# Six layers of windowed attention on one core: both halves of the product with V in one block, and K's projection split around P's transposes

## The chip, the cores and the metric

The kernel runs on one core of a Trainium2 chip. The metric is the device time in microseconds of one execution; lower is better. Times are medians of the runs named. Engines are called TensorE (PE; PEld is its weight load), VectorE (DVE), ScalarE (ACT), GpSimd (POOL) and SyncE (SP, which here only issues DMAs).

## The reference, cut to what matters

The input is x of shape (4, 512, 128), float32. First comes a full attention with 16 heads of 64 and a residual, then a second residual around six layers, each a windowed attention and a gated FFN:

```python
x = x + attn(layernorm(x), Wq, Wk, Wv, Wr)          # 16 heads, full softmax over 512 keys
h = layernorm(x)
for i in range(6):
    t = shift_tokens(h)                              # half of the features come from the token before
    q, k, v = split(t @ Wqkv[i])                     # 128 -> 3 x 1024
    q, k = rotary(l2norm(q) * qs[i]), rotary_inv(l2norm(k) * ks[i])
    p = softmax(8 * q @ k2.T + band)                 # windows of 32 queries, 64 keys: own window and the one before
    h = (p @ v2) @ Wo[i] + h                         # 1024 -> 128
    t = layernorm(shift_tokens(h)) * g + b
    a, gate = split(t @ W1[i] + b1)                  # 128 -> 2 x 341
    h = (a * gelu(gate)) @ W2[i] + b2 + h
x = x + h
```

## The kernel before

There are two stages in one program, with instruction order on every engine written out by hand. The first stage (to about 568 us) is the full attention; the change does not touch it. The second stage is the six layers.

**Units and slots.** A unit is 128 tokens of one layer: 6 layers x 4 batch entries x 4 tiles = 96 units, numbered in that order. Activations lie transposed, features on partitions. The work is a software pipeline: `slot(n)` emits, in this order, parts of four units: scores and the exponential of unit n; the projections, rotation and norms of unit n+2 (`new`); the transposes of Q and K of unit n+1 (`nxt`); and the output projection and residual of unit n-1 (`prev`). The FFN of a finished batch entry (four units) is spread over the following seven slots in three lists, `move` (the token shift), `norm` (mean, variance, scale, one a slot) and `geglu` (three chunks of 128 of the inner width, then the output). After unit n-1, with n a multiple of four, the shift is in slot n, the mean in n+1, the variance in n+2, the scale in n+3, the chunks in n+3 to n+5, the output in n+6.

**One slot on TensorE before.** Scores: eight bf16 matmuls that lay the band mask (L652), then 128 float32 matmuls of 64x32 tiles (L663). Q's projection (L517; one half of 512 columns is two matmul records in the trace). The norm's step, if the slot has one (L97, L106 or L114). Output projection of the unit before (L720, 16 records). P's eight transposes in two groups of four (L625, from `pr`). K's projection. First half of the product with V (`times_v(u, 0)`, L695, 64 matmuls of 64x32 tiles). Q's eight transposes (L625, from `rot`). V's projection. Second half of the product (`times_v(u, 1)`). K's eight transposes. The FFN's chunk (L763, L764) or output (L783). The eight transposes of the product (L625, from `on`).

**The other engines.** VectorE reduces the scores to maxima (L673) and subtracts them (L675), adds the residual (L728), rotates Q and K in two operations each (L538, L542), sums their squares (L533) and divides the product by the softmax sums (L704, L705, once per half). ScalarE does the exponential (L681), the squares (L528), all copies of transposes out of PSUM (L628), V's copies (L607) and the FFN's gelu (L767). GpSimd adds the two parts of a rotation (L553), scales Q and K by their inverse norms (L561) and does the Newton steps of inverse roots (L84 to L87); the two integer operations that start a root (L81, L82) are on VectorE. SyncE issues sixteen copies per unit which spread V into windows (L615 to L619), used two slots later.

**PSUM.** Three tiles of two banks, `two0` to `two2`, and two tiles of one bank, taken in turn by `one_t`. `two_t(k)` takes tile (part + k) mod 3, and `part` is set at the start of every slot:

```python
part[0] = n % 3
```

In a slot, scores take k=0, Q's projection 1, K's 2, both halves of the product 0, V's projection 1, the FFN 2. `one_t` serves, in turn: the norm's step, the output projection's y, P's two groups, Q's two, K's two, the product's two. With two such tiles, P's second group takes the one that held y, which L728 must have read.

Of the kernel before, what the change touches and what calls it, by code (L numbers as in the profile page):

```python
# [15 lines left out]
P = 128  # L16
# [16 lines left out]
def body(ctx: ExitStack, tc: tile.TileContext, a, out: bass.AP):  # L33
# [54 lines left out]

    def layernorm_steps(state, bank, inT, outT, g=None, b=None, eng=nc.vector, nt=NT, temp=tmpt):

        w = nt * P

        def mean():
            m = bank()[:, 0:w]
            mm(m, lhsT=avg, rhs=inT(), start=True, stop=True)  # L97
            xc = state["xc"] = temp()[:, 0:w]
            nc.vector.tensor_tensor(xc, inT(), m, ALU.subtract)
            sq = state["sq"] = temp()[:, 0:w]  # L100
            nc.scalar.activation(sq, xc, AF.Square)

        def var():
            v = bank()
            for t in range(nt):
                mm(v[:, t : t + 1], lhsT=state["sq"][:, t * P : (t + 1) * P], rhs=avg[:, 0:1], start=True, stop=True)  # L106
            rs = state["rs"] = small.tile([P, NT], F32, tag="rs", name="rs")[:, 0:nt]
            nc.vector.tensor_scalar(rs, v[:, 0:nt], EPS, None, ALU.add)  # L108
            rsqrt(rs, nt, eng)

        def scale():
            bc = bank()[:, 0:w]
            for t in range(nt):
                nc.tensor.transpose(  # L114
                    bc[:, t * P : (t + 1) * P], state["rs"][:, t : t + 1].to_broadcast([P, P]), ident
                )
            h = state["h"] = outT()
            nc.vector.tensor_tensor(h, state["xc"], bc, ALU.mult)
            if g is not None:
                nc.vector.tensor_scalar(h, h, g, b, ALU.mult, ALU.add)  # L120

        return mean, var, scale
# [390 lines left out]

    def project(u, j):
        p = two_t((1, 2, 1)[j], "ps_proj")
        for c in range(2):
            mm(  # L517
# [5 lines left out]
            )  # L523
        return flat(p)

# [8 lines left out]

    def rotate(u, j):
        t0 = u.r[j] = s2a.tile([P, INNER], F32, tag="rot", name="rot", bufs=6)
        lt, pf, half = u.lt, u.p[j], HD // 2
        nc.vector.tensor_tensor(  # L538
            heads(t0), heads(pf), lt[:, u.T, 2 * j].unsqueeze(1).to_broadcast([P, HEADS, HD]), ALU.mult
        )  # L540
        t1 = u.t1 = s2a.tile([P, INNER], F32, tag="t1", name="t1", bufs=3)
        nc.vector.tensor_tensor(  # L542
# [139 lines left out]

    def transpose_p(u):
        u.pT = s2.tile([P, NC, P], F32, tag="pT", name="pT", bufs=2)
        for g in range(2):
            transposed(u.prf, g, u.pT, 0)

    def times_v(u, g, k=0):
        if g == 0:
            u.on = s2.tile([P, NC, 2, HD], F32, tag="on", name="on", bufs=1)  # L690
        o = two_t(k, "ps_att")
        for c in range(4):
# [40 lines left out]
    class Ffn:  # L733
        def __init__(self, u, t0=0, nt=NT, temp=tmpt, pair=None, eng=None):
            self.i, self.b, self.u, self.t0, self.nt, self.us, self.st = u.i, u.b, u, t0, nt, [], {}
# [9 lines left out]
                nt,  # L745
                temp,
            )

# [84 lines left out]

    def do_project(u, j):
        u.p[j] = project(u, j)
        if u.b + 1 == B and u.T + 1 == NT and u.i + 1 < L:
            wpart[j] = load_part(u.i + 1, j)
# [25 lines left out]
    def slot(n, norm, move, geglu):  # L863
# [4 lines left out]
        u, prev, nxt, new = unit(n), unit(n - 1), unit(n + 1), unit(n + 2)  # L868
        part[0] = n % 3
        begin(unit(n + 4))  # L870
# [16 lines left out]
        for f in move:  # L887
            f()
        if u:
            transpose_p(u)  # L890
        if new:
# [5 lines left out]
        if new:  # L897
            do_project(new, 1)
            square(new, 1)
        if u:  # L900
            times_v(u, 0)
        if nxt:
            transpose_q(nxt)
        if new:
            do_project(new, 2)
            v_windows(new, follower(new))
            rotate(new, 1)
            add_rotated(new, 1)
        if u:
            times_v(u, 1)  # L910
        if new:
            sum_squares(new, 1)
        if nxt:
# [14 lines left out]
    with tc.manual_schedule():  # L928
        begin(units[0])
        late = norm_x1(one_t, B - 1)  # L930


        norm, move, geglu = {}, {}, {}

# [7 lines left out]
        for n in range(NT, end - NT, NT):  # L942
            f = Ffn(units[n - 1], eng=nc.gpsimd)
            plan(move, n, f.shift)
            for k, g in enumerate((f.mean, f.var, f.scale)):
                plan(norm, n + 1 + k, g)
            for k in range(3):
                plan(geglu, n + 3 + k, at(f.chunk, k, 2))
            plan(geglu, n + 6, at(f.out, 2, n + 6 == end - 2))
        third, seq = f, Ffn(units[end - NT - 1], eng=nc.gpsimd)  # L950
# [26 lines left out]
        def tail():  # L977
# [5 lines left out]
            most.shift()  # L983
            transpose_p(u)
            most.mean()
            part[0] = 1
            times_v(u, 0, 0)
            times_v(u, 1, 1)
            part[0] = 0
# [26 lines left out]
        for n in range(-1, end - 1):  # L1016
            if 1 <= n < 4:
                late[n - 1]()
            slot(n, norm.get(n, ()), move.get(n, ()), geglu.get(n, ()))
# [94 lines left out]
```

## Time and profile before

| | |
|---|---|
| three runs | 2259.30, 2260.88, 2263.07 us; median 2260.88 |
| profiled execution | 2261.35 us; its span from first to last instruction 2259.6 us |
| granted TensorE clock | 0.993 of full speed |
| TensorE busy in the span | 2183.4 us |
| VectorE, ScalarE, GpSimd busy | 1710.3, 1365.9, 1511.7 us |
| slots of the layers (start of one L652 to the next) | 96 from 568.5 us on; usual lengths 16.3, 17.2, 18.5, 17.0 us for n mod 4 = 0, 1, 2, 3 |

The profile is one execution. A row of its order of time gives start, busy time, engine, line, operation, the tiles written and read, shape and count, and in brackets how long the engine was idle before and what ended it. Matmuls overlap one another in the pipe and their ends are modelled, so for TensorE the distance from one start to the next says more than the busy time.

### The profile page before, as it was taken

To read this page: it belongs to the slowest core of one execution; us is meant where nothing else is said; L and a number is where in the kernel's file an instruction comes from. 1 tells how busy PE (TensorE), PEld (TensorE's weight loads), DVE (VectorE), ACT (ScalarE), POOL (GpSimd) and SP (SyncE) were. 2 spreads that over 40 slices of the span, in tenths; PEclk is the share of its full clock that TensorE was granted. 3 is DMA by queue.
4 is the path that set the end of the run, shared out by engine and by line. 5 is a ranking of instruction groups with operands and counts; after the bars stand their busy time and mean duration, and the time that the engine had idled before them with its cause. 6 is when DMAs were issued, how large, how long until landed. Compare 5 with 4: busy or idle time off the path is not lost.

```text
span 2259.6 us, 82472 instructions
## 1 busy us (share of the span) xinstructions
PE 2183.4 (97%) x35150; PEld 1435.4 (64%) x35150; DVE 1710.3 (76%) x2501; ACT 1365.9 (60%) x2589; POOL 1511.7 (67%) x2281
## 2 busy tenths in 40 slices
PE   7999999999899999999999999999999999999997
PEld 5565655554666666666666666666666666666665
DVE  4676667676778888878788788878888788888874
ACT  4665656564556656666566656666566666666663
POOL 2554545465787777777777777777777777777762
PEclk8999999999999999999999999999999999999999
DMA  3000000000322233232322323223232223322221
GB/s 117 1 1 1 1 1 1 1 1 9 75 69 60 69 87 73 57 76 69 85 69 62 78 66 86 66 67 73 71 85 63 66 71 87 76 63 70 60 67 28
DMA packets 91064, 125.77 MB, mean 56 GB/s; under 512 B 25422, under 2 KB 39500, under 8 KB 90700
## 3 DMA queue, kind: packets, MB, share of 16 engines
q1 hardware_dynamic: 89996, 118.79, 21.4%
q8 instruction: 280, 4.59, 0.9%
q10 hardware_dynamic: 704, 1.70, 0.2%
q14 instruction: 84, 0.69, 0.1%
HBM read 20.31 MB, written 1.05 MB: 9 GB/s over the span
## 4 chain that ended last, share of the span: by engine, by line
PE 58%; DVE 12%; POOL 3%; issue 2%; ACT 1%; POOLq 0%; ACTq 0%
PE ps_proj L517 18%; PE ps_one L625 14%; PE ps_att L663 6%; PE ps_att L695 6%; PE ps_one L720 3%; PE ps_proj L783 3%; PE ps_proj L763 3%; PE ps_proj L764 3%; DVE y L82 2%; DVE mx L673 2%; DVE pr L675 2%; PE ps_att L652 1%; DVE hT L120 1%; POOL rot L553 1%; DVE t L542 1%
## 5 line engine op out<-in xcount | busy, mean ns | idle before, releaser
L553 POOL TENSOR_TENSOR rot<-rot,t 128x1024 f32<-128x1024 f32 x192 | 453.9, 2365 | 255.8 <-DVE t L542 188.5
L517 PE MATMUL ps_proj<-wqkv,xs 128*128 128x512 f32 x1152 | 557.0, 606 | 5.9 <-DVE tmp_t L771 5.0
L344 POOL TENSOR_TENSOR pr<-pr,den 128x1024 f32<-128x1024 f32 x128 | 241.0, 1894 | 247.5 <-DVE den L341 239.6
L561 POOL TENSOR_TENSOR rot<-rot,ss 128x1024 f32<-128x1024 f32 x192 | 361.5, 1904 | 7.4
L517 PEld LDWEIGHTS ps_proj<-wqkv,xs 128*128 128x128 f32 x1152 | 197.5, 191 | 157.2 <-issue 143.2
L528 ACT ACTIVATE sq<-ps_proj 128x1024 f32<-128x1024 f32 x192 | 195.3, 1017 | 127.5 <-PE ps_proj L517 126.8
L681 ACT ACTIVATE pr<-pr 128x1024 f32<-128x1024 f32 x96 | 101.5, 1058 | 260.8 <-DVE pr L675 260.8
L542 DVE TENSOR_TENSOR t<-ps_proj,lt 128x1024 f32<-128x1024 f32 x192 | 233.2, 1215 | 19.6 <-POOL rot L553 19.2
L538 DVE TENSOR_TENSOR rot<-ps_proj,lt 128x1024 f32<-128x1024 f32 x192 | 233.0, 1214 | 19.5 <-ACT sq L528 19.4
L533 DVE TENSOR_REDUCE ss<-sq 128x16 f32<-128x1024 f32 x192 | 231.6, 1206 | 0.0
L330 ACT ACTIVATE pr<-ps_sc,nm 128x128 f32<-128x128 f32 (+3 forms) x448 | 220.6, 511 | 5.7 <-DVE nm L317 5.2
L317 DVE TENSOR_REDUCE nm<-ps_sc 128x2 f32<-128x1024 f32 x128 | 155.9, 1218 | 82.8 <-PE ps_sc L305 82.7
L673 DVE TENSOR_REDUCE mx<-ps_att 128x16 f32<-128x1024 f32 x96 | 117.5, 1224 | 127.1 <-PE ps_att L663 127.1
L625 PE MATMUL ps_one<-ident,rot 128*128 128x128 f32 x1536 | 209.6, 279 | 0.9 <-POOL rot L561 0.9
L720 PEld LDWEIGHTS ps_one<-aT,wo 128*128 128x128 f32 x1536 | 183.0, 192 | 24.6 <-issue 23.9
L720 PE MATMUL ps_one<-aT,wo 128*128 128x128 f32 x1536 | 189.1, 276 | 0.4 <-DVE rs L108 0.3
L625 PEld LDWEIGHTS ps_one<-ident,rot 128*128 128x128 f32 x1536 | 164.7, 141 | 19.8 <-POOL rot L561 1.1
L695 PEld LDWEIGHTS ps_att<-vw,pT 64*32 64x32 f32 x9216 | 101.1, 105 | 108.3 <-issue 108.0
L607 ACT COPY vt<-ps_proj 128x512 f32<-128x512 f32 x192 | 103.2, 590 | 101.3 <-PE ps_proj L517 101.3
L355 PEld LDWEIGHTS ps_pt<-ident,pr 128*128 128x128 f32 x1024 | 118.2, 142 | 56.9 <-issue 47.1
L84 POOL TENSOR_TENSOR yt<-y 128x32 f32<-128x32 f32 (+2 forms) x384 | 88.0, 229 | 93.6 <-DVE y L82 47.5
L355 PE MATMUL ps_pt<-ident,pr 128*128 128x128 f32 x1024 | 135.7, 275 | 3.0 <-POOL pr L344 2.7
(173 smaller groups left out, 4083.0 us busy)
## 6 DMA issues: line engine op xcount, KB each, us to landing
vw<-vt SPq DMA_DIRECT2D x1152, 65.0 KB, 2.0
vw_first<-vt SPq DMA_DIRECT2D x336, 65.0 KB, 2.0
wqkv<-in_wqkv_dram SPq DMA_DIRECT2D x18, 512.0 KB, 9.2
wo<-in_wo_dram SPq DMA_DIRECT2D x6, 512.0 KB
w<-in_w_dram SPq DMA_DIRECT2D x6, 341.0 KB, 3.5
xr<-in_x_dram SPq DMA_DIRECT2D x3, 256.0 KB
scales<-in_scales_dram SPq DMA_DIRECT2D x6, 128.0 KB, 3.2
w<-in_w_dram SPq DMA_DIRECT2D x12, 64.0 KB, 2.9
```

Source lines behind the costliest of these rows:

```text
L330: nc.scalar.activation(self.pr[:, h, cols], self.sc[:, h, cols], AF.Exp, bias=self.nm[:, part_, h : h + 1], accum_out=self.den[:, part_, h ...
L344: nc.gpsimd.tensor_tensor(self.pr, self.pr, self.den[:, 0].unsqueeze(2).to_broadcast([P, 2, S]), ALU.mult)
L355: nc.tensor.transpose(pt[:, k * P : (k + 1) * P], self.pr[:, h, k * P : (k + 1) * P], ident)
L517: mm(p[:, c, :], lhsT=u.xs[:, u.T * P : (u.T + 1) * P], rhs=wpart[j][:, c * 512 : (c + 1) * 512], start=True, stop=True,)
L533: nc.vector.tensor_reduce(u.ss[:, j * HEADS : (j + 1) * HEADS], heads(u.sq), AX.X, ALU.add)
L538: nc.vector.tensor_tensor(heads(t0), heads(pf), lt[:, u.T, 2 * j].unsqueeze(1).to_broadcast([P, HEADS, HD]), ALU.mult)
L542: nc.vector.tensor_tensor(t1.rearrange("p (h t d) -> p h t d", t=2, d=half), pf.rearrange("p (h t d) -> p h t d", t=2, d=half)[:, :, ::-1, :],
L553: nc.gpsimd.tensor_tensor(u.r[j], u.r[j], u.t1, ALU.add)
L561: nc.gpsimd.tensor_tensor(heads(u.r[j]), heads(u.r[j]), u.ss[:, j * HEADS : (j + 1) * HEADS].unsqueeze(2).to_broadcast([P, HEADS, HD]), AL ...
L625: nc.tensor.transpose(tp[:, c * P : (c + 1) * P], src[:, (4 * g + c) * P : (4 * g + c + 1) * P], ident)
L695: mm(o[j * W : (j + 1) * W, h, c * (HD + 1) : (c + 1) * (HD + 1)], lhsT=u.pT[h * HD : (h + 1) * HD, 4 * g + c, j * W : (j + 1) * W], rhs=u ...
L720: mm(y[:, 0:P], lhsT=wo_w[0][:, c, :], rhs=u.aT[:, c, :], start=(c == 0), stop=(c == NC - 1))
```

## The change

Nine things change, all in the layers' stage; no arithmetic is added or left out.

1. K's projection is split into its two halves of 512 columns. One half is emitted ahead of P's second group of transposes (in slots with no norm step ahead of both groups), the other behind them. In slot 0 the whole of it comes ahead.
2. Both halves of the product with V are emitted one after the other, into tiles 0 and 1 of the slot.
3. V's projection, which stood between them, comes behind them and behind Q's transposes, into tile 0, the tile of the product's first half. K's rotation (VectorE) comes ahead of it in the text, behind the product's division.
4. The tiles turn the other way: `part` is (-1 - n) mod 3, and the FFN takes tile 1 instead of 2.
5. Three operations of the FFN's norm, the square (L101), the root (L81 to L87) and the gain and offset (L120), are put on a list and emitted between the two operations that rotate K.
6. The norm of the last batch entry ahead of the layers is emitted inside slots 0, 1 and 2 rather than ahead of slots 1, 2 and 3.
7. The sum of K's squares comes directly behind K's rotation.
8. In the last layer the transposes and the store of a finished batch entry come one slot after the FFN's output rather than directly behind it.
9. In slot 0, Q's transposes come ahead of the product.

```diff
-        p = two_t((1, 2, 1)[j], "ps_proj")
-        for c in range(2):
+    def project(u, j, c0=0, c1=2):
+        p = u.p[j] if c0 else two_t(((1, 2, 1), (0, 2, 1), (1, 2, 0))[min(u.n, 2)][j], "ps_proj")
+        u.p[j] = p
+        for c in range(c0, c1):
...
-    def rotate(u, j):
+    def rotate(u, j, between=()):
...
+        for f in between:
+            f()
         t1 = u.t1 = s2a.tile([P, INNER], F32, tag="t1", name="t1", bufs=3)
...
-            nc.scalar.activation(sq, xc, AF.Square)
+            then(lambda: nc.scalar.activation(sq, xc, AF.Square))
...
-            rsqrt(rs, nt, eng)
+            then(lambda: rsqrt(rs, nt, eng))
...
-                nc.vector.tensor_scalar(h, h, g, b, ALU.mult, ALU.add)
+                then(lambda: nc.vector.tensor_scalar(h, h, g, b, ALU.mult, ALU.add))
...
-        part[0] = n % 3
+        part[0] = (-1 - n) % 3
...
+        if n == 0:
+            do_project(new, 1)
         if u:
-            transpose_p(u)
+            if norm:
+                transpose_p(u, 0)
+        if new and n != 0:
+            do_project(new, 1, 0, 1)
+        if u:
+            if not norm:
+                transpose_p(u, 0)
+            transpose_p(u, 1)
         if new:
             rotate(new, 0)
             add_rotated(new, 0)
...
         if new:
-            do_project(new, 1)
+            if n != 0:
+                do_project(new, 1, 1)
             square(new, 1)
+        if nxt and n == 0:
+            transpose_q(nxt)
         if u:
             times_v(u, 0)
-        if nxt:
+            times_v(u, 1)
+        if new:
+            rotate(new, 1, later)
+            later.clear()
+            add_rotated(new, 1)
+            sum_squares(new, 1)
+        if nxt and n != 0:
             transpose_q(nxt)
         if new:
             do_project(new, 2)
             v_windows(new, follower(new))
-            rotate(new, 1)
-            add_rotated(new, 1)
-        if u:
-            times_v(u, 1)
-        if new:
-            sum_squares(new, 1)
         if nxt:
             transpose_k(nxt)
...
-                plan(geglu, n + 3 + k, at(f.chunk, k, 2))
-            plan(geglu, n + 6, at(f.out, 2, n + 6 == end - 2))
+                plan(geglu, n + 3 + k, at(f.chunk, k, 1))
+            ends = f.i + 1 == L
+            plan(geglu, n + 6, at(f.out, 2 if n + 6 == end - 2 else 1, ends))
+            if ends and n + 6 < end - 2:
+                plan(geglu, n + 7, f.finish)
```

In `times_v` the tile is now `two_t(g, "ps_att")`, g being the half.

More of the change, by code (lines that the diff above doesn't have):

```diff
@@ L87, in rsqrt, with layernorm_steps, then @@
             eng.tensor_tensor(y if k < 2 else v, y, t, ALU.mult)
-    def layernorm_steps(state, bank, inT, outT, g=None, b=None, eng=nc.vector, nt=NT, temp=tmpt):
+    def layernorm_steps(state, bank, inT, outT, g=None, b=None, eng=nc.vector, nt=NT, temp=tmpt, later=None):
         w = nt * P
+        def then(f):
+            f() if later is None else later.append(f)
         def mean():
@@ L512, in __init__ @@
             self.r = [None, None]
-    def project(u, j):
-        p = two_t((1, 2, 1)[j], "ps_proj")
-        for c in range(2):
+    def project(u, j, c0=0, c1=2):
+        p = u.p[j] if c0 else two_t(((1, 2, 1), (0, 2, 1), (1, 2, 0))[min(u.n, 2)][j], "ps_proj")
+        u.p[j] = p
+        for c in range(c0, c1):
             mm(
@@ L523, in project @@
             )
-        return flat(p)
+        if c1 == 2:
+            u.p[j] = flat(p)
     def square(u, j):
@@ L681, in exponents, with transpose_p, times_v @@
         nc.scalar.activation(u.prf, u.prf, AF.Exp)
[L683 to L688, printed above, removed]
+    def transpose_p(u, g):
+        if g == 0:
+            u.pT = s2.tile([P, NC, P], F32, tag="pT", name="pT", bufs=2)
+        transposed(u.prf, g, u.pT, 0)
+    def times_v(u, g):
         if g == 0:
             u.on = s2.tile([P, NC, 2, HD], F32, tag="on", name="on", bufs=1)
-        o = two_t(k, "ps_att")
+        o = two_t(g, "ps_att")
         for c in range(4):
@@ L733, in body, with __init__ @@
     class Ffn:
-        def __init__(self, u, t0=0, nt=NT, temp=tmpt, pair=None, eng=None):
+        def __init__(self, u, t0=0, nt=NT, temp=tmpt, pair=None, eng=None, later=None):
             self.i, self.b, self.u, self.t0, self.nt, self.us, self.st = u.i, u.b, u, t0, nt, [], {}
@@ L746, in __init__ @@
                 temp,
+                later,
             )
@@ L832, in begin, with do_project @@
             v.xs, v.lt, v.p = xs, lt, [None] * 3
-    def do_project(u, j):
-        u.p[j] = project(u, j)
-        if u.b + 1 == B and u.T + 1 == NT and u.i + 1 < L:
+    def do_project(u, j, c0=0, c1=2):
+        project(u, j, c0, c1)
+        if c1 == 2 and u.b + 1 == B and u.T + 1 == NT and u.i + 1 < L:
             wpart[j] = load_part(u.i + 1, j)
@@ L929, in body @@
         begin(units[0])
+        later = []
         late = norm_x1(one_t, B - 1)
-        norm, move, geglu = {}, {}, {}
+        norm, move, geglu = {k: [f] for k, f in enumerate(late)}, {}, {}
         def plan(steps, n, *fs):
@@ L942, in body @@
         for n in range(NT, end - NT, NT):
-            f = Ffn(units[n - 1], eng=nc.gpsimd)
+            f = Ffn(units[n - 1], eng=nc.gpsimd, later=later)
             plan(move, n, f.shift)
@@ L983, in tail @@
             most.shift()
-            transpose_p(u)
+            transpose_p(u, 0)
+            transpose_p(u, 1)
             most.mean()
             part[0] = 1
-            times_v(u, 0, 0)
-            times_v(u, 1, 1)
+            times_v(u, 0)
+            times_v(u, 1)
             part[0] = 0
@@ L1016, in body @@
         for n in range(-1, end - 1):
-            if 1 <= n < 4:
-                late[n - 1]()
             slot(n, norm.get(n, ()), move.get(n, ()), geglu.get(n, ()))
```

## Prediction

> **What bounds the kernel now.** I read the engine totals first, then the waits, then TensorE's own order of time in one layer slot.
>
> The page's totals, and its TensorE rows over 40 slices:
>
> ```profile
> PE 2183.4 (97%) x35150; PEld 1435.4 (64%) x35150; DVE 1710.3 (76%) x2501; ACT 1365.9 (60%) x2589; POOL 1511.7 (67%) x2281
> ...
> PE   7999999999899999999999999999999999999997
> PEld 5565655554666666666666666666666666666665
> ```
>
> TensorE is full from end to end; nothing else is near it. So a change that removes no arithmetic gains only what TensorE loses between instructions. Those losses do not show as idle time, because a matmul's record runs on while the pipe empties. I therefore count from start to start. TensorE in order of time (start, busy, line, count, idle before and who ended it), one slot of 17.02 us, from L652 up to the FFN's first half (eight transposes of the product, 0.97 us, end it):
>
> ```profile
> 1311.90 0.41 PE L652 MATMUL ps_att<-band,ident 64*32 64x512 bf16 x8
> 1312.12 1.72 PE L663 MATMUL ps_att<-kT,qT 64*32 64x64 f32 x128
> 1313.77 1.98 PE L517 MATMUL ps_proj<-wqkv,xs 128*128 128x512 f32 x4
> 1315.59 0.60 PE L114 MATMUL ps_one<-ident,rs 128*128 128x128 f32 x4
> 1316.03 1.95 PE L720 MATMUL ps_one<-aT,wo 128*128 128x128 f32 x16
> 1317.81 0.60 PE L625 MATMUL ps_one<-ident,pr 128*128 128x128 f32 x4
> 1318.67 0.66 PE L625 MATMUL ps_one<-ident,pr 128*128 128x128 f32 x4 [0.26 <-DVE xT L728]
> 1319.16 1.88 PE L517 MATMUL ps_proj<-wqkv,xs 128*128 128x512 f32 x4
> 1320.98 0.86 PE L695 MATMUL ps_att<-vw,pT 64*32 64x65 f32 x64
> 1321.77 1.09 PE L625 MATMUL ps_one<-ident,rot 128*128 128x128 f32 x8
> 1322.70 1.88 PE L517 MATMUL ps_proj<-wqkv,xs 128*128 128x512 f32 x4
> 1324.51 0.86 PE L695 MATMUL ps_att<-vw,pT 64*32 64x65 f32 x64
> 1325.30 1.09 PE L625 MATMUL ps_one<-ident,rot 128*128 128x128 f32 x8
> 1326.23 1.02 PE L763 MATMUL ps_proj<-hT,w 128*128 128x512 f32 x2
> 1327.09 1.02 PE L764 MATMUL ps_proj<-hT,w 128*128 128x512 f32 x2
> ```
>
> Two losses are seen. First, P's eight transposes take 1.35 us (1317.81 to 1319.16), while four of L114 take 0.44, so eight should take 0.88. Second, each block of 64x32 tiles (L695) costs something at both ends: four projection matmuls take 1.82 us ahead of it and 1.72 elsewhere (L763 with L764), and the eight transposes behind it take 0.93 instead of 0.88.
>
> Who delays P: the same stretch on VectorE and GpSimd (first three rows one slot earlier), and the totals by waiter (us, times, longest):
>
> ```profile
> 1298.62 1.91 POOL L561 TENSOR_TENSOR rot<-rot,ss 128x1024 f32<-128x1024 f32 x1
> 1298.71 1.83 DVE L82 TENSOR_SCALAR y<-yt 128x4 int32<-128x4 int32 x1
> 1300.46 0.28 DVE L728 TENSOR_TENSOR xT<-ps_one,xT 128x128 f32<-128x128 f32 x1
> ...
> 1317.15 1.27 DVE L120 TENSOR_SCALAR hT<-hT,vecs 128x512 f32<-128x512 f32 x1
> ```
>
> ```profile
> PEld ps_one L625 <- DVE xT L728: 32.6, 69, 1.7
> ...
> PE ps_one L625 <- DVE xT L728: 17.5, 44, 1.4
> ```
>
> The second four of P need the bank that holds y until L728 has added the residual. L728 stands on VectorE behind the norm's little operations, and L82 on 128x4 took 1.83 us because it ended with GpSimd's L561; elsewhere it takes 0.18.
>
> **The change part by part.** Classes are slots by n mod 4: class 1 does the norm's mean, 2 its variance and the FFN's output, 3 its scale, 0 no norm. S is a slot's start, E the end of its L720 block.
>
> *P's wait.* Over 95 slots, start to start, P's blocks and the steps into them exceed 0.11 us per transpose by 8.1 us in class 0, 4.0 in class 1, 16.7 in class 2, 11.2 in class 3: 40.1 in all. Class 0 is another wait: P comes 0.26 us ahead of the exponential's end (S+5.61). Afterwards half of K's projection (two matmuls at 0.43, 0.86 us) stands ahead of P's second four, and in class 0 ahead of P altogether. L82 and L120 are behind L728 now, so L728 ends near E+0.5, and P's second four come at E+1.30. Covered everywhere, by 0.8 us; class 0's exponential by 0.7. Minus 40.1 us. Splitting K removes no matmul and repeats none, so the split itself is nothing.
>
> *One block.* This takes away one switch into small tiles and one out. Into: 0.523 against 0.429 us from the last projection matmul, 0.094. Out: the first transpose step takes 0.165 against 0.109, 0.056. The two blocks take 0.79 each from first to follower; how a joint block runs is to be seen once, in the tail of before:
>
> ```profile
> 2227.94 1.59 PE L695 MATMUL ps_att<-vw,pT 64*32 64x65 f32 x128
> 2229.46 1.12 PE L763 MATMUL ps_proj<-hT,w 128*128 128x512 f32 x2
> ```
>
> That is 1.52 for 1.58, 0.063. Together 0.213 us by 95 slots, minus 20.2. The Trainium skill, "TensorEngine Tiling (Array Packing)", Key Properties, says that a change of tiling mode drains the engine. By that rule alone I would price the switch at what a matmul's record has left after its follower's turn: 0.592-0.429 in, and 0.217-0.010 out, 0.37 a slot, minus 35. The rows show cheaper switches, and the joint block in the tail stands for itself; I take 20.2, and keep 6 (a joint block as slow as scores, 1.65) to 35 as ends.
>
> The Trainium skill's "Perfetto Trace Analysis", Identifying the Most-Contended Engine, calls matmul busy share a bad measure of room on TensorE. This bears on the sum: idle time by the busy rows is 196 of each 200 us, 2% of the 1650 us of layers, so at most 33 us; the start-to-start count finds 60. I use the latter.
>
> *V behind the product, tiles turned.* V's projection goes into the tile of the product's first half, so it waits for that half's division (L704, L705). TensorE after E: P 0.44, K 0.86, P 0.44, K with the switch 0.95, the product 1.52, Q's transposes 0.93: V is due at E+5.14. VectorE from L538 on: steps of 1.15, 1.13, 1.13, 0.23 and L705's 0.69, 4.33 us. L538 starts at E+0.4 in classes 1 and 2, so L705 ends at E+4.75: no wait. In class 3 L538 starts at S+6.64, E+0.73: E+5.06, just in time. In class 0 L538 cannot start before ScalarE's square of the same tile ends (S+6.55, E+1.03): E+5.36, with 0.05 for the signal and 0.1 for an exposed weight load 0.37 us late, 24 times: plus 8.9. The product's second half needs L542 of Q done, at E+3.1 to E+3.4, and is due at E+3.41: nothing. Turning the tiles the other way puts scores on the tile of the previous K (L542 done by E+8.5, scores at E+10.4), Q on the previous V's, K on the FFN's: all released earlier than needed; the waits of L517 for L771 (5 us on PE) are included in P's margin.
>
> *The rest of the moved work.* L120 now stands between K's two rotations, in class 3 at E+6.95; GpSimd is between its two L553 then, so it should take the 0.55 us of its shortest record on 128x512 rather than the usual 1.37, and end at E+7.5; the FFN's first matmul is due at E+7.73. If it were blocked again: 0.6 us in 23 slots, 14 us; I keep that for the range. The norm's root on GpSimd (12 small operations, 3.3 us) now delays K's L553 and so the next unit's scaling by up to 3 us in class 2; Q's transposes still have over 2 us. V's projection moves from E+4.9 to E+5.1, so the sixteen window copies on SP's queue (0.5 to 1.3 us each, wanted two slots later) move by as little. At a layer's start the scales' load stands behind them and lt's product holds GpSimd; slots 45 and 61 took 20.8 and 21.5 us for 17.2. With shorter slots this bites earlier: nothing to 2 us at each of five starts, I take 4 in all. The final transposes moved out of slot 90 (21.58 us for 18.4 in its class; four transposes come back in slot 91): minus 2.5. In slot 0 K's whole projection fills part of a 2.3 us wait for the exponential: minus 1.5.
>
> Sum: -40.1-20.2+8.9+4-2.5-1.5 = -51.4. The profiled execution is 2261.35 us (span 2259.6), 0.5 above the median of the three runs, 2260.88: 2209.5.
>
> **The rivals.**
> *VectorE's ring takes over* (21 in 100). Per slot VectorE is busy about 14 us of 17, and L557 will now be blocked behind K's L553 for about 1 us, where a division stood before. If it is late by 0.3 us per slot at scores or at V, 28 us come back: 2237. For it: its margin before scores falls from 1.1 to 0.2-0.5 us by the rows. Against: it now idles 127.1 us in all for scores.
> *Nothing comes back* (10 in 100): class 0's wait doesn't show and a joint block costs less: 2190.
> *V waits for the whole product* (7 in 100), the slower side. If V is released only by the second half's L705 (0.95 us later: E+5.7 to E+6.3), it is 0.6 to 1.3 us late in every slot, with the load about 1.0, 95 us: 2296. The break-even is a new wait of 0.68 us per slot (64.3/95). Against it: VectorE runs in order, and the first half's L705 is counted first.
>
> **How the numbers follow.** My forecast has 62 in 100, 2196 to 2224 by itself. The range takes in most of the second and third case: 2191 to 2240. This kernel's runs tell 0.2% apart, 4.5 us; only the slower case or part of the second reaches there: faster 0.90, same 0.03, slower 0.07.
>
> **What would show it.** P's two groups of four at 0.44 us each without a wait for the residual; one block of 128 L695 matmuls of about 1.5 us; slots of 16.3, 16.8, 17.5, 16.3 us by class; a VectorE wait ahead of V's projection in class 0 only. Wrong if that wait is in all classes, if FFN matmuls wait for hT, or if slots keep their length.

## The result and the profile after

Before: 2261.57 us (2259.30 to 2263.07). After: 2227.98 us (2223.71 to 2230.22). The ratio is 0.9853, with a 95% interval of 0.9840 to 0.9867: 33.6 us less, where the forecast said 51.4. The profiled execution of after took 2230.15 us, its span 2228.3.

The page's totals of after, and TensorE's rows over 40 slices:

```profile
PE 2153.5 (97%) x35150; PEld 1438.0 (65%) x35150; DVE 1704.1 (76%) x2501; ACT 1358.5 (61%) x2589; POOL 1510.9 (68%) x2281
...
PE   7999999999889999999999999999999999999997
PEld 5555655555566666666666666666666666666665
```

The number of matmuls is the same, and TensorE is as full as before, so the 31.3 us of span have gone from between its instructions, as the forecast wanted. (After's line numbers are higher: band L659, scores L670, projections L521, output projection L727, transposes L632, product L702, FFN L771, L772 and L791; on VectorE maxima L680, rotation L543 and L549, sums L538, division L711 and L712, residual L735.) TensorE in order of time, in after, from P's first group to V's projection; a slot of class 3, the same slot number 43 as shown of before:

```profile
1303.32 0.60 PE L632 MATMUL ps_one<-ident,pr 128*128 128x128 f32 x4
1303.76 1.02 PE L521 MATMUL ps_proj<-wqkv,xs 128*128 128x512 f32 x2
1304.62 0.60 PE L632 MATMUL ps_one<-ident,pr 128*128 128x128 f32 x4
1305.06 1.02 PE L521 MATMUL ps_proj<-wqkv,xs 128*128 128x512 f32 x2
1306.01 1.74 PE L702 MATMUL ps_att<-vw,pT 64*32 64x65 f32 x128
1307.68 1.09 PE L632 MATMUL ps_one<-ident,rot 128*128 128x128 f32 x8
1308.61 1.89 PE L521 MATMUL ps_proj<-wqkv,xs 128*128 128x512 f32 x4
```

P's groups are 0.44 us from start to follower (1303.32 to 1303.76, 1304.62 to 1305.06) with no wait behind either; before, the two took 1.35 together here. The product is one block. Here it took 1.67 us with its follower; its median in this class is 1.45.

The same rows in the next slot, class 0:

```profile
1319.31 1.02 PE L521 MATMUL ps_proj<-wqkv,xs 128*128 128x512 f32 x2
1320.17 1.04 PE L632 MATMUL ps_one<-ident,pr 128*128 128x128 f32 x8
1321.05 1.02 PE L521 MATMUL ps_proj<-wqkv,xs 128*128 128x512 f32 x2
1322.00 1.87 PE L702 MATMUL ps_att<-vw_first,pT 64*32 64x65 f32 x128
1323.80 1.09 PE L632 MATMUL ps_one<-ident,rot 128*128 128x128 f32 x8
1324.98 1.99 PE L521 MATMUL ps_proj<-wqkv,xs 128*128 128x512 f32 x4
```

Two new losses are seen without any bracket: the product takes 1.80 us instead of 1.44, and Q's eight transposes 1.18 (1323.80 to 1324.98) instead of 0.93. The totals of the waits of after on TensorE:

```profile
PE ps_att L702 <- issue: 11.8, 10, 2.7
PE ps_att L670 <- issue: 8.8, 10, 1.9
...
PE ps_one L632 <- DVE xT L735: 1.4, 1, 1.4
```

P's wait for the residual, 17.5 us in 44 places before, is one place of 1.4 us. New on top is a wait of the product for "issue", nothing that the profile shows; before it had 0.9 us, once.

From start to start, summed by operation over slots 0 to 94 (us):

| operation | before | after |
|---|---|---|
| P's transposes | 115.8 | 86.6 |
| output projection | 174.4 | 171.2 |
| projections of Q, K, V | 517.7 | 508.0 |
| product with V | 153.3 | 163.2 |
| transposes of Q and K | 181.9 | 194.7 |
| scores | 164.0 | 155.5 |
| the rest (norm, FFN, other transposes, band) | 342.0 | 334.5 |
| sum | 1649.1 | 1613.7 |

That is -35.4; the first scores begin 2.7 us later than before (571.2 for 568.5) and the tail is 1.5 us longer. A typical slot, taken as the sum of the medians of its operations (so were the lengths given of before), has 16.40, 16.86, 17.49 and 16.31 us in classes 0 to 3, where the forecast said 16.3, 16.8, 17.5 and 16.3. The whole slots have medians of 16.42, 17.00, 17.50 and 16.33 and means of 16.43, 17.14, 17.63 and 16.74: the typical slot was forecast well, and something irregular was not.

### The profile page after: what moved, and what is told of

It is laid out like the page before. It is cut to its first block, busy times and chain, and to the rows that moved or that the text cites. A ratio compares the mean times of both kernels' runs of the same rounds, so it can differ in the third digit from the quotient of the medians.

```text
span 2228.3 us, 82460 instructions
## 1 busy us (share of the span) xinstructions
PE 2153.5 (97%) x35150; PEld 1438.0 (65%) x35150; DVE 1704.1 (76%) x2501; ACT 1358.5 (61%) x2589; POOL 1510.9 (68%) x2281
## 4 chain that ended last, share of the span: by engine, by line
PE 50%; DVE 14%; POOL 6%; issue 4%; ACT 2%; POOLq 0%; ACTq 0%
PE ps_proj L521 15%; PE ps_one L632 10%; PE ps_one L727 5%; PE ps_att L670 5%; PE ps_att L702 4%; DVE t L549 3%; DVE ss L538 3%; PE ps_proj L791 3%; PE ps_proj L771 2%; PE ps_proj L772 2%; DVE rot L543 2%; POOL rot L568 2%; POOL rot L560 2%; DVE pr L682 1%; DVE mx L680 1%
## 5 line engine op out<-in xcount | busy, mean ns | idle before, releaser
L560 POOL TENSOR_TENSOR rot<-rot,t 128x1024 f32<-128x1024 f32 x192 | 454.1, 2367 | 198.7 <-DVE t L549 165.8
L521 PE MATMUL ps_proj<-wqkv,xs 128*128 128x512 f32 x1152 | 573.6, 607 | 5.2 <-issue 1.6
L568 POOL TENSOR_TENSOR rot<-rot,ss 128x1024 f32<-128x1024 f32 x192 | 361.6, 1905 | 7.5
L521 PEld LDWEIGHTS ps_proj<-wqkv,xs 128*128 128x128 f32 x1152 | 189.5, 191 | 122.3 <-issue 102.8
L543 DVE TENSOR_TENSOR rot<-ps_proj,lt 128x1024 f32<-128x1024 f32 x192 | 233.8, 1218 | 31.3 <-ACT sq L533 31.0
L549 DVE TENSOR_TENSOR t<-ps_proj,lt 128x1024 f32<-128x1024 f32 x192 | 233.5, 1216 | 29.4 <-POOL rot L560 29.4
L538 DVE TENSOR_REDUCE ss<-sq 128x16 f32<-128x1024 f32 x192 | 232.0, 1208 | 0.0
L632 PEld LDWEIGHTS ps_one<-ident,rot 128*128 128x128 f32 x1536 | 173.0, 141 | 66.7 <-issue 53.9
L632 PE MATMUL ps_one<-ident,rot 128*128 128x128 f32 x1536 | 206.1, 277 | 6.3 <-issue 2.1
L727 PEld LDWEIGHTS ps_one<-aT,wo 128*128 128x128 f32 x1536 | 184.4, 193 | 23.7 <-issue 23.0
L727 PE MATMUL ps_one<-aT,wo 128*128 128x128 f32 x1536 | 190.7, 278 | 0.4 <-DVE rs L111 0.3
L680 DVE TENSOR_REDUCE mx<-ps_att 128x16 f32<-128x1024 f32 x96 | 117.3, 1222 | 74.4 <-PE ps_att L670 74.3
L635 ACT COPY qT<-ps_one 128x512 f32<-128x512 f32 x192 | 103.5, 589 | 111.7 <-PE ps_one L632 111.7
L635 ACT COPY pT<-ps_one 128x512 f32<-128x512 f32 x192 | 109.9, 586 | 75.3 <-PE ps_one L632 75.1
```

The source lines that it names most:

```text
L521: mm(p[:, c, :], lhsT=u.xs[:, u.T * P : (u.T + 1) * P], rhs=wpart[j][:, c * 512 : (c + 1) * 512], start=True, stop=True,)
L538: nc.vector.tensor_reduce(u.ss[:, j * HEADS : (j + 1) * HEADS], heads(u.sq), AX.X, ALU.add)
L543: nc.vector.tensor_tensor(heads(t0), heads(pf), lt[:, u.T, 2 * j].unsqueeze(1).to_broadcast([P, HEADS, HD]), ALU.mult)
L549: nc.vector.tensor_tensor(t1.rearrange("p (h t d) -> p h t d", t=2, d=half), pf.rearrange("p (h t d) -> p h t d", t=2, d=half)[:, :, ::-1, :],
L560: nc.gpsimd.tensor_tensor(u.r[j], u.r[j], u.t1, ALU.add)
L568: nc.gpsimd.tensor_tensor(heads(u.r[j]), heads(u.r[j]), u.ss[:, j * HEADS : (j + 1) * HEADS].unsqueeze(2).to_broadcast([P, HEADS, HD]), AL ...
```

## Where the new losses are

**The division of the product's first half.** V's projection waits for its tile, and that for L712 on VectorE. In class 0 (VectorE in order of time, after, slot 44, which starts at 1313.90):

```profile
1320.52 1.23 DVE L543 TENSOR_TENSOR rot<-ps_proj,lt 128x1024 f32<-128x1024 f32 x1 [0.71 <-ACT sq L533]
1321.66 1.22 DVE L549 TENSOR_TENSOR t<-ps_proj,lt 128x1024 f32<-128x1024 f32 x1
...
1324.15 0.69 DVE L712 TENSOR_TENSOR on<-ps_att,rden 128x512 f32<-128x512 f32 x1
```

L543 starts late, behind ScalarE's square (the bracket). The product's second half needs L549's tile, and L549 ends at 1322.88, 0.88 us into a product that began at 1322.00: its second 64 matmuls, due after some 0.72, stand. L712 ends at 1324.84, and V starts at 1324.98. In medians over the class: 0.36 in the product, 0.25 behind Q's transposes, 0.07 in V's first weight load, 0.68 us a slot.

In class 1 the cause is one slot earlier. VectorE of after, the end of slot 36 and slot 37 (which starts at 1195.08):

```profile
1192.83 1.23 DVE L549 TENSOR_TENSOR t<-ps_proj,lt 128x1024 f32<-128x1024 f32 x1 [1.27 <-POOL rot L560]
...
1195.21 1.39 DVE L564 TENSOR_SCALAR ss<-ss 128x32 f32<-128x32 f32 x1
...
1197.07 0.74 DVE L779 SCALAR_TENSOR_TENSOR tmp_t<-ps_proj,vecs,tmp_t 128x512 f32<-128x512 f32 x1
1197.73 1.21 DVE L680 TENSOR_REDUCE mx<-ps_att 128x16 f32<-128x1024 f32 x1
...
1202.24 1.23 DVE L543 TENSOR_TENSOR rot<-ps_proj,lt 128x1024 f32<-128x1024 f32 x1 [0.29 <-ACT sq L533]
...
1205.87 0.69 DVE L712 TENSOR_TENSOR on<-ps_att,rden 128x512 f32<-128x512 f32 x1
```

K's second rotation L549 waited 1.27 us for GpSimd's add L560, which stood behind two token shifts (1187.61 to 1190.35): the next units' and the FFN's, both in slots of class 0. So the operations behind it come late: L564, which takes 1.38 or 1.39 us beside GpSimd's next L560 in classes 0 to 2 alike (medians), starts 0.1 us into the slot in class 1, against 0.8 and 1.2 ahead of it in classes 0 and 2. The gate L779 runs into the new slot, and the maxima begin 2.65 us into it instead of about 2.07. The exponential, the square behind it and so L543 come late; L712 ends at 1206.56, and V, which was due 0.93 us behind the start of Q's transposes (1205.58 + 0.93 = 1206.51), starts at 1206.71. In medians 0.27 us a slot. Class 3 loses 0.19, since the joint block is faster than forecast and V is due sooner. Class 2 loses nothing. Together 0.68 x 24 + 0.27 x 24 + 0.19 x 23 = 27.2 us, by medians.

**Stops inside a run of small matmuls.** TensorE of after, two product blocks:

```profile
1508.86 1.46 PE L702 MATMUL ps_att<-vw,pT 64*32 64x65 f32 x122
1513.05 0.43 PE L702 MATMUL ps_att<-vw,pT 64*32 64x65 f32 x6 [2.73 <-issue]
...
1886.46 1.31 PE L702 MATMUL ps_att<-vw,pT 64*32 64x65 f32 x105
1889.45 0.43 PE L702 MATMUL ps_att<-vw,pT 64*32 64x65 f32 x23 [1.68 <-issue]
```

In the middle of a block (before matmul 123, before matmul 106) the engine stands for 1.9 to 3 us with no semaphore to wait for. Counting every gap of over 0.3 us between two matmuls of one block: in the product 1.1 us before (one place), 16.9 after (19 places; nine of them are class 0's wait for L549 at the half, 0.31 to 0.36 each, two are of 0.4 and 0.5, the other eight are over 0.6); in the scores 8.1 and 11.0. What these stops are is taken up behind the experiments.

## The experiments

The theory (A) after the result: P's wait and the joint block pay as forecast, and the rest is lost to VectorE's later division and to stops of TensorE in the joint block. The rivals are named in the expectations. Each ratio is to runs of before made along with that version. A difference from after is taken between medians made at different times; reckoned through the two ratios it comes out up to 3 us otherwise.

**K's split alone.** Before, with K's halves around P's second group and nothing else:

```diff
+        if u and norm:
+            transpose_p(u, 0)
+        if new:
+            do_project(new, 1, 0, 1)
         if u:
-            transpose_p(u)
+            if not norm:
+                transpose_p(u, 0)
+            transpose_p(u, 1)
...
-            do_project(new, 1)
+            do_project(new, 1, 1)
```

> The kernel before with K's projection split around P's transposes and nothing else: tiles, product, V and norm stay as before. Theory A (P's waits are worth about 35 us by themselves, and what the rest of the change gains at the small-tile switches, some 28 us, is lost again to waits on VectorE ahead of the product's second half and of V, and to TensorE running out of instructions in the joint block): this alone takes 2261 to about 2228, as fast as the whole change, with P's two groups at 0.44 us each. Theory B (the wait for the residual only moves to the next step that needs VectorE, so the split is worth less than 20 us and the joint block brings the rest): 2242 or more.

Measured: 2252.85 us (2247.13 to 2254.07), ratio 0.9966 [0.9952, 0.9980]. What A says of the split alone fell here; B was right. P's groups do take 0.44 us, yet little comes of it. TensorE, then VectorE, of this kernel in a slot of class 0 (here the FFN is L765, K's second rotation operation L544, GpSimd's add L555):

```profile
1269.34 1.09 PE L627 MATMUL ps_one<-ident,rot 128*128 128x128 f32 x8
1271.32 1.12 PE L765 MATMUL ps_proj<-hT,w 128*128 128x512 f32 x2 [0.89 <-DVE t L544]
```

```profile
1270.04 1.23 DVE L544 TENSOR_TENSOR t<-ps_proj,lt 128x1024 f32<-128x1024 f32 x1 [1.08 <-POOL rot L555]
```

The FFN takes K's tile in the old order of tiles, so it waits until K's second rotation operation has read it, and that waits for GpSimd's add of Q. TensorE is earlier, GpSimd is not, and the time comes back 0.89 us at a stretch, 12.4 us in 18 places.

**The norm's operations moved, alone.** Before, with only the three operations put between K's rotations:

```diff
-            f = Ffn(units[n - 1], eng=nc.gpsimd)
+            f = Ffn(units[n - 1], eng=nc.gpsimd, later=later)
...
-            rotate(new, 1)
+            rotate(new, 1, later)
+            later.clear()
```

> The kernel before with one part of the change: the norm's square, root and gain are emitted between the two operations that rotate K; P, the product, V and the tiles stay as before. Theory E (most of P's wait was the residual's add standing behind these operations on VectorE while GpSimd held them up; once they are away it is 0.17 us per slot): P's blocks fall from 1.56 and 1.37 us to about 1.04 in slots 2 and 3 mod 4, about 0.85 us per four slots, 20 us: 2240. Rival F (the later rotation of K holds the FFN's tile, and the gain comes back there): 2250 or more.

Measured: 2253.90 us (2250.50 to 2265.97), ratio 0.9972 [0.9957, 0.9986]. P's eight transposes fell to 1.04 us in classes 1 to 3, and class 0's FFN waited for the same operation (L547 there; K's transposes with the wait 1.48 us for 0.93). F was right.

**The full change without K's split.** After, with all of K behind P:

```diff
         if u:
-            if norm:
-                transpose_p(u, 0)
-        if new and n != 0:
-            do_project(new, 1, 0, 1)
-        if u:
-            if not norm:
-                transpose_p(u, 0)
+            transpose_p(u, 0)
             transpose_p(u, 1)
...
-                do_project(new, 1, 1)
+                do_project(new, 1)
```

> The changed kernel with K's projection whole again behind both groups of P's transposes. Theory A: P's second group waits for the residual (about 0.17 us in three of four slots, 0.31 us for the exponential in the fourth, 19 us in all), but V then comes later by as much and waits less for VectorE, so the net is about +10: 2238. Theory B: the split is worth little: 2228 to 2233.

Measured: 2230.04 us (2225.51 to 2233.71), ratio 0.9871 [0.9849, 0.9893], which overlaps the interval of after, as theory B said. P's transposes take 1.04 us in classes 1 to 3, and class 0 waits some 0.3 us for the exponential again; but the product takes 1.44 us in class 0, and in class 3 Q's transposes are back at 0.93. What P gains by the split, the division takes at V.

**The full change without the moved norm.** After, with the three operations in their old place:

```diff
-            f = Ffn(units[n - 1], eng=nc.gpsimd, later=later)
+            f = Ffn(units[n - 1], eng=nc.gpsimd)
```

> The changed kernel with the norm's square, root and gain at their old places, ahead of the residual. Theory A: K's half still covers the residual's delay, VectorE comes 0.1 to 0.4 us later to the product in one or two slots of four and V waits that much more: 2230 to 2236. Rival C (putting them between K's rotations lengthens VectorE's and GpSimd's ring and makes the new waits): faster than the changed kernel, 2222 or less.

Measured: 2250.41 us (2246.18 to 2260.63), ratio 0.9964 [0.9955, 0.9973]. The expectation was wrong: 22 us of the change hang on this move (25 by the ratios). VectorE, then TensorE, in a slot of class 2 of this kernel:

```profile
1224.95 1.67 DVE L81 TENSOR_SCALAR yt<-rs 128x4 int32<-128x4 int32 x1
1226.65 1.82 DVE L82 TENSOR_SCALAR y<-yt 128x4 int32<-128x4 int32 x1
1228.39 0.28 DVE L735 TENSOR_TENSOR xT<-ps_one,xT 128x128 f32<-128x128 f32 x1
```

```profile
1226.88 1.02 PE L521 MATMUL ps_proj<-wqkv,xs 128*128 128x512 f32 x2
1228.72 0.66 PE L632 MATMUL ps_one<-ident,pr 128*128 128x128 f32 x4 [0.82 <-DVE xT L735]
```

L81 and L82 on 128x4 take 1.67 and 1.82 us beside GpSimd's L568 (1224.69 to 1228.45), the residual ends at 1228.67, 2.23 us behind the output projection's end, and half of K covers 0.86 of that. In class 2 this costs 0.6 us at P and 0.25 each in the product and behind Q's transposes, medians. In after the same two operations stand between K's rotations and take 0.16 and 0.17.

**A shorter sum of squares.** After, with Q's sum over 16 of the 64 features of each head, so that L712 comes sooner; this kernel leaves out three quarters of Q's squares:

```diff
-        nc.vector.tensor_reduce(u.ss[:, j * HEADS : (j + 1) * HEADS], heads(u.sq), AX.X, ALU.add)
+        sq = heads(u.sq)[:, :, 0 : HD // 4] if j == 0 else heads(u.sq)
+        nc.vector.tensor_reduce(u.ss[:, j * HEADS : (j + 1) * HEADS], sq, AX.X, ALU.add)
```

> The changed kernel with the sum of Q's squares taken over 16 of 64 features per head (this leaves out part of the computation), so that VectorE reaches the product's division about 0.88 us earlier. Theory A, its VectorE part: V's waits of 0.32, 0.26 and 0.19 us in slots with n mod 4 = 0, 1, 3 go, 18 us, and the late start of the scores' maxima in slots 1 mod 4 eases: about 2208. If the shortfall were TensorE's instruction supply alone (rival D): 2228, unchanged.

Measured: 2210.51 us (2209.50 to 2217.13), ratio 0.9787 [0.9769, 0.9805]. Q's transposes take 0.93 us in every class, V waits nowhere, and 17.5 us are gone (15 by the ratios), where V's waits by medians are 18.6. So the waits of V are lost time of TensorE, at about their full length. Class 0's product stayed at 1.80 us, as it must, since L549 is ahead of the sum.

**Q's transposes between the halves.** After, with Q's transposes moved from behind the product to between its two halves:

```diff
         if u:
             times_v(u, 0)
+        if nxt and n != 0:
+            transpose_q(nxt)
+        if u:
             times_v(u, 1)
...
-        if nxt and n != 0:
-            transpose_q(nxt)
```

> The changed kernel with Q's transposes between the two halves of the product, so that no run of 128 product matmuls stands together. Theory G (TensorE uses up instructions faster than they are fetched when 128 of these matmuls stand in one run): the irregular stops inside the product, some 13 us in the changed kernel's profile, fall to 1 or 2, and the wait of the second half for Q's rotation (0.31 us in every fourth slot, 7 us) goes; the second pair of switches costs 0.29 us per slot, 27 us, and V comes 0.15 us nearer to VectorE's time: together near no change, 2222 to 2234. If the stops are not tied to the run's length they stay near 13 us and the time rises by 15 or more: 2243.

Measured: 2234.32 us (2230.68 to 2239.12), ratio 0.9884 [0.9863, 0.9905], the upper edge of what was expected. The switch in and out of small tiles is paid again (27.6 us by the count below), but the stops shrink: 3.3 us in the product for 16.9, and 11.0 for 31.9 with those in scores and behind the blocks, counted as in the last section. The two make +6.7; measured are +6.3. This kernel's waits:

```profile
PE ps_att L670 <- issue: 5.0, 5, 1.4
...
PE ps_att L702 <- issue: 1.9, 5, 0.6
```

**The square first.** After, with ScalarE's square of Q ahead of the exponential (L543 waits for the square), the exponential's table loaded by an activation on 128x2 behind the scores, and K's first half ahead of both groups of P in all slots:

```diff
             scores(u)
-            exponents(u)
+            early_table()
         if new:
             do_project(new, 0)
             square(new, 0)
+        if u:
+            exponents(u)
...
-            if norm:
-                transpose_p(u, 0)
...
-            if not norm:
-                transpose_p(u, 0)
+            transpose_p(u, 0)
             transpose_p(u, 1)
```

> The changed kernel with ScalarE's square of Q ahead of the exponential of the scores, the exponential's table called up early by a tiny activation at the exponential's old place, and the first half of K's projection ahead of both groups of P in every slot. Theory A, its VectorE part (VectorE cannot start Q's rotation before that square has read the tile, and the square stands behind the exponential): the rotation starts 0.4 to 0.7 us earlier, and the waits ahead of the product's second half and V, 0.68, 0.29 and 0.19 us in slots 0, 1, 3 mod 4, go: about 2205. If VectorE is held by its own load instead: 2222 to 2230.

Measured: 2224.64 us (2222.65 to 2232.38), ratio 0.9846 [0.9825, 0.9868]: a miss, in the rival's range, but not for its reason. V waits in no class any more and class 0 fell to 15.82 us, but the product took 1.64 to 1.66 in classes 1 to 3.

**The square first, P in its place.** The same without the last part, so that P's first group is ahead of K's first half where a slot has a norm step:

> The changed kernel with ScalarE's square of Q ahead of the exponential (and the exponential's table loaded right behind the scores by an activation on a 128x2 tile), but with P's first group where the changed kernel has it, ahead of K's first half in the slots with a norm step. The square-first run had lost its gain in classes 1 to 3 where the product's second half waited (1.64 us for 1.44). Theory: that wait came from K's half standing ahead of both groups of P, so with P's first group back in its place the product takes 1.44 in classes 1 and 2, class 0 stays at 15.8 to 15.9 us, class 1 falls from 16.86 to 16.58, class 3 to 16.1: (0.5+0.28+0.2) x 23.75 = 23 us, 2205 us; 2204 to 2213. Rival: the wait came from the later exponential itself, so P's first group now waits for it and the gain stays at some 3 us: 2221 to 2228.

Measured: 2210.39 us (2207.39 to 2217.02), ratio 0.9776 [0.9757, 0.9795], as the theory said, and the best version that keeps the whole computation. TensorE around the product in one slot of class 1 (number 41), of the kernel with both groups behind K's half and then of this one:

```profile
1269.49 1.87 PE L706 MATMUL ps_att<-vw,pT 64*32 64x65 f32 x128
1271.29 0.44 PE L632 MATMUL ps_one<-ident,rot 128*128 128x128 f32 x2
```

```profile
1271.10 1.53 PE L706 MATMUL ps_att<-vw,pT 64*32 64x65 f32 x128
1272.56 0.55 PE L632 MATMUL ps_one<-ident,rot 128*128 128x128 f32 x3
```

1.80 us from product to follower in the first, 1.46 in the second (medians of this class 1.66 and 1.45). So the place of P's first group decides it. That the half of K between P's groups gives ScalarE time for its copy of the first group would explain it; the traces show no wait that says so. The typical slots are 15.81, 16.70, 17.48 and 16.22 us in classes 0 to 3. By these, 0.59 x 24 + 0.16 x 24 + 0.01 x 24 + 0.09 x 23 = 20.3 us less than after; the times say 17.6.

**Units started later.** After, with the token shift of a unit (GpSimd) and its loads emitted one slot later, `begin(unit(n + 3))` for `n + 4`:

> The changed kernel with the token shift and the tables of the next four units emitted one slot later, away from the slot in which GpSimd already does the FFN's shift. Theory A: GpSimd's part of K's rotation in slots 0 mod 4 comes 1.3 us earlier, the scores' maxima in slots 1 mod 4 start at 2.1 instead of 2.6 us, and V's wait of 0.26 us there goes: 2221. If that lateness has another cause: 2228.

Measured: 2228.05 us (2224.26 to 2234.62), ratio 0.9858 [0.9835, 0.9881]. Class 1's wait for V went, as expected (typical slot 16.58 us for 16.86, maxima 2.07 us into the slot), so the two token shifts in one slot are the cause of it. The total did not move: the stops in the product rose from 16.9 to 21.9 us, with three new ones of 1.3 to 1.7 us in slots of class 1 itself, and class 2's mean slot rose by 0.13 us, 3.0 us in all.

**Both.** The square-first kernel with P in its place, and units started later:

> The kernel above with the start of a unit (the shift of its tokens and their loads) one slot later, n+3 for n+4. The square ahead of the exponential already takes class 1's wait for V away, which is all that the later shift took away by itself. Theory: nothing added, within 5 us of the kernel above. Rival (the later shift also frees VectorE for class 1's maxima, and both waits had been there together): 8 us or more below it.

Measured: 2215.46 us (2212.53 to 2221.27), ratio 0.9800 [0.9780, 0.9820]: nothing added, as the theory said; it is 5.1 us above the kernel without the later start, and the two intervals overlap.

**Tiles forward again.** After with `part[0] = n % 3` in place of `(-1 - n) % 3`, nothing else:

> The changed kernel, but the tiles turn forward again (part = n mod 3); nothing else. With k = 0, 1, 2 for scores, Q and K, tile 0 of the slot is then the one that the FFN's chunk (k=1 of the slot before) has just filled, so the scores of a slot wait until the FFN's gate has been read (line 779). In the changed kernel that reader ends 1.8, 2.7 and 1.5 us into the next slot in classes 0, 1 and 2. Theory (turning is what lets the other parts pay): scores in classes 0, 1 and 2 start 1.5 to 2.7 us late, +110 to +150 us, about 2350 us, well slower than the kernel before. Rival (the turn is slack, since the gate's reader would run earlier when TensorE stands still, and the maxima of VectorE absorb the rest): below 2240 us.

Measured: 2354.19 us (2350.41 to 2359.72), ratio 1.0413 [1.0392, 1.0433], on the theory's number. Its waits have a new first row, and its TensorE shows one place of it at the start of a slot of class 1:

```profile
PE ps_att L659 <- DVE tmp_t L779: 118.3, 66, 5.3
```

```profile
1314.02 0.41 PE L659 MATMUL ps_att<-band,ident 64*32 64x512 bf16 x8 [1.46 <-DVE tmp_t L779]
```

So the turn is not slack: with V behind the product in one block, the old direction puts scores on the tile that the FFN has just filled.

## Why the prediction was right, and where its sizes were off

The time fell as forecast and lies 18.5 us above the predicted one. By its own steps:

| step | forecast | found |
|---|---|---|
| P's wait, slot 0 with it | -41.6 | about -35 |
| joint block, without new waits | -20.2 | -27.6 |
| new waits at V and at the product's second half | +8.9 | +27.2 |
| stops without a semaphore, in and right behind product and scores | 0 | +22.7 |
| scores, apart from stops and the starts of layers | 0 | about -7 |
| starts of layers | +4 | about -8 |
| the end of the layers (slot 90) | -2.5 | about -3 |
| first scores later, tail longer | 0 | +4.2 |

The right column adds up to -26 of the span's -31.3; the rest is spread over many small differences and is not assigned. That the forecast came so near is in part luck: +18 at V and +23 of stops were not in it, and against them stand gains that were not in it either, 7 at the block, 12 at the starts of layers and 7 in scores. What made scores faster stays open; part of it is that there are 90 small breaks (0.05 to 0.25 us between two matmuls) in the blocks of after and 153 in those of before.

*P's wait.* Right, a little too large. The transposes lost 29.2 us, the output projection ahead of them 3.3, slot 0 some 2.4. Slots 0 and 94 keep 2.9 us at P, and 2.0 us of the step into P in class 2 (0.08 a slot) are there before and after, so they were no part of P's wait. That K's half covers the residual "everywhere, by 0.8 us" held because L82 and L120 were moved; the runs show how the two share it. Without the move 22 us come back, without the split about 2, which these runs can't tell from nothing.

*The joint block.* Right in kind, too small. The product is 1.44 us up to its follower when nothing stops it, not the 1.52 of the tail of before. So 0.14 by the block, 0.094 on the switch in, 0.056 on the switch out, 0.29 x 95 = 27.6. It lies between the forecast's 20.2 and the 35 that it had worked out from the draining rule of the Trainium skill ("TensorEngine Tiling (Array Packing)", Key Properties). The count from start to start also proved the better measure of room: the kernel with the shorter sum and the square-first kernel with P in its place took 49 and 50 us off, with stops still in them, more than the 33 that the idle time by the busy rows would have allowed. (The 196 of each 200 us that the forecast calls idle there are the busy time; its 2% is right.)

*V behind the product.* The step that failed. The forecast had the wait in class 0 only, at 0.37 us a slot; it is in classes 0, 1 and 3, and 27.2 us in all. Three terms were mis-sized. In class 0 "the product's second half needs L542 of Q done ... nothing" had no margin: the rotation was to start at E+1.03, starts at E+1.20 (median) and ends at E+3.56 where the half is due at E+3.41, and 0.36 is lost. In class 3 the division ends at E+5.05, as forecast, but "just in time" was reckoned with a product of 1.52 us; one of 1.44 makes V due 0.08 earlier, and the 0.15 for the signal and the exposed weight load, charged in class 0 alone, comes on top. In class 1 L538 (now L543) was to start at E+0.4, and that rested on maxima at their old time; behind GpSimd's two token shifts they come 0.6 us later than before, and L543 starts at E+0.79. This is the first rival, VectorE's ring, which was given 0.3 us per slot; the mean over the slots is 0.29. It came about at V, not at scores. That the 128x32 operation would be blocked for about 1 us, as that rival said, is so (L564 1.38 us, before 0.35, medians), but only in class 1 does it cost anything.

*Stops without a semaphore.* The second term that was far off: the forecast had nothing for them, nor a rival that named them, and they are 22.7 us. What they are stands in the last section.

*The rest.* The moved gain and offset (now L123) took 0.54 us where 0.55 was said, and no FFN matmul waits for it. The starts of layers went the other way: slots 45 and 61 took 20.84 and 21.46 us before, 16.58 and 16.88 after. TensorE of before in slot 45:

```profile
1349.11 3.68 PE L517 MATMUL ps_proj<-wqkv,xs 128*128 128x512 f32 x4 [1.75 <-DVE tmp_t L771]
```

Q's projection stood there for the FFN's tile. With the tiles turned it takes another one, and the wait is gone from both slots. The forecast had counted those waits into P's margin and still added 4 us.

*The third rival* (V waits for the whole product) is excluded: in class 2 V waits for nothing. *The slower side* does exist in this change, but in the turn of the tiles, which the forecast called early enough without a price: left out, it costs 126 us.

*What single parts are worth.* K's split alone gives 6.5 us, the norm's move alone 7.5. The full change gives 33.6, and taking the norm's move out of it costs 22 to 25. A part whose gain is caught by the next wait is worth more once another part has taken that wait away.

## What to carry to other kernels

Where one engine is full, price the removal of a wait by what is due next behind it: a part tried alone can show little, and the same part taken out of the whole shows what it carries. When a tile is given to a later user, count the readers of each tile from the trace with the new start times, the faster ones too, and take a margin under 0.1 us as a wait. And on an in-order engine put what is ready and awaited (here the square) ahead of what still waits for its input (the exponential).

## What the runs showed of the hardware

*Stops without a semaphore.* 128 matmuls of a product and their 128 weight loads are 256 instructions, done in 1.44 us. The larger instruction queue in all these profiles moves 280 packets of 16,384 bytes. After has 70,300 matmuls and loads, and 71,763 records of TensorE with its semaphore waits: 256 for each packet. So this queue is TensorE's by its size, and such a block uses up one packet.

Counted so in order of time, the stops are not spread at random: in all thirteen kernels each one of over 0.4 us in a product or in scores comes in front of record 193, 194 or 195 of a run of 256, while class 0's waits for L549 stand anywhere. Of 252 such places in the layers of after, TensorE is held up by more than 0.25 us beyond its usual step at 28, by 31.9 us together (one more, of 0.28, had its packet 5 us earlier and is another wait): 13.9 in the product, 10.9 in scores, 7.1 in what follows right behind a block. Before it is 9.2 us in 12 places, with transposes between the halves 11.0 in 15. Whether a place is hit depends on its packet: at all 28 it ended less than 1.2 us before the matmul was due, or later than that time, and at all but two of the other 223 it had ended more than 1.2 us ahead. TensorE goes on 1.3 to 1.6 us behind the packet's end: of the two stops shown, the packets ended at 1511.60 and 1888.11, and TensorE went on at 1513.05 and 1889.45. At stops of over 0.6 us the packet took 0.88 to 1.29.

The Trainium skill, "Runtime: NRT & Kernel Launch", Instruction fetch mechanics, has instructions come in blocks of 16 KiB, 256 instructions, and calls the cost of crossing one mostly hidden. The size agrees; hidden it is not where a block's end falls late in a dense run of small matmuls, and the joint product makes such runs longer. This leaves little room for another cause than the fetch, but no run changed the fetch itself, and what starts a packet stays open. It also limits what can be told from small shifts: the sum went from 31.9 to 25.6 us in square-first with P in its place and to 38.2 in short-sum, by no design of the edits.

*Small operations beside GpSimd.* L82 on 128x4 took 1.82 us beside a GpSimd operation on 128x1024 and 0.17 between K's rotations in after; L564 on 128x32 took 1.39 beside one and 0.18 at the least. It is not their own work that makes them dear, so where they stand in the order of VectorE decides.
